# Raw sums of a scan's chunks on two column tiles, with six rearranging transfers per chunk

## The chip, the cores and the metric

The kernel runs on one core of a Trainium2 chip. The metric is the device time of one execution in microseconds, as the median of several runs. The core has TensorE (PE, whose weight loads are listed as PEld), VectorE (DVE), ScalarE (ACT), GpSimd (POOL) and SyncE (SP). SP and ACT issue the DMA transfers.

## The reference, cut to what matters

The input `x` is 32 sequences of 256 positions of 256 values. The output is `x + FFN(COND(x))`. `FFN` is two layers of windowed attention and a gated feed-forward part. `COND` is a state-space block, and the change lies in it:

```
xr, gate = split(x @ W_in.T);  xc = silu(conv4(xr + cond))
xn = layernorm(xc) * ln_g + ln_b                  # per position, 512 channels
Bm, Cm, dt = split(xn @ W_xproj.T, 3)             # 16 states each
dt = tanh(dt @ W_dt.T + b_dt) * 0.01;  Ad = 1 - dt * tanh(A_log)
Bd = Bm * min(norm(xn), 1)
h  = clip(h * Ad + Bd * xn, -10, 10)              # one step per position
y  = sum over states of Cm * h + D * xn
out = (y * silu(gate)) @ W_out.T
```

## The kernel before

The 32 sequences go in four groups of 8 (`GB`). A group's scan runs over 256 positions in 8 chunks of 32 steps (`CH`), so there are 32 chunks in all. On the partitions lie 16 states times 8 sequences, and `step` (line 719) does one position of all of them with one VectorE instruction of 128x512. Before it, `load_rows` (L688) loads the position's normalised rows, repeated over the 16 states, from DRAM into `xrep` on SP's queue, and `scale_row` (L708) scales them by `beta` on ScalarE, two steps ahead. `read_out` (L729) multiplies four steps' `h` on four 32-column tiles of TensorE into `y`.

What a chunk needs ahead of its steps is prepared about a chunk earlier. `conv_in` to `conv_out` make `xc`, which holds 512 channels as four blocks of 128 partitions, with 8 sequences times 32 steps as 256 columns. Three things follow from `xc`:

- `raw_sums` (L517) multiplies it with the 64 columns of `wx_sb` (16 each for Bm, Cm and dt, and 16 of zeros), in four fp32 matmuls of 256 columns, one per block of channels, each recorded as two passes. `raw_copy` (L526) copies the 64x256 sums from PSUM to `raw` on ScalarE. `raw_turn` (L531) brings them with three transfers on ScalarE's queue into `rw`, which has states times sequences on the partitions and three rows of 32 steps.
- `norm_turn` (L542) to `norm_put` transpose `xc`, normalise it and store it to DRAM as `xnd`, which `load_rows` reads back.
- `figures` and `figures_out` bring each position's scale, shift and norm to the layout of `rw`. `figures_in` (L633) is the first reader of `rw`: it makes `bcd` and `beta`. `decays` makes the running products, the limits and the read-out weights.

Group 0 runs its scan almost alone. Beside it TensorE projects the inputs of the other three groups ahead (`ahead_project`, L423, with `ps_a`) and spreads some rows itself (`spread_rows`, L693, with `bx`). From then on each group's scan runs beside attention and feed-forward of the group before it. After the last scan only attention and feed-forward are left. `values` (L1281) of the attention computes `ov` with 64-column weights, two heads alternating between the lower and the upper 64 output partitions; its products have 256 columns for the first window of keys and 128 for the second. `sums` (L1263) uses four 32-column tiles.

The source writes down an order. A table of slots, one per step, says which function is called in which slot:

```
at(s0 - 25, raw_copy, c)
at(s0 - 24, raw_turn, c)
...
at(s0 - 7, figures_in, c)
...
at(s0 - 27, raw_sums, c)
```

Here `s0` is the chunk's first step. The framework then orders the instructions of each engine by its own plan, except for those marked `keep_in_program_order`, and adds the waits. All eight PSUM banks form one ring (`ps_w`, `bufs=8`), from which every matmul output takes a bank. `raw` has one buffer and `rw` has two. A second form of the program (`exact`) is chosen only for large attention scales and does not run here.

Of the kernel before, what the change touches and what calls it, by code (L numbers as in the profile page):

```python
# [10 lines left out]
FP = mybir.dt.float32  # L11
# [8 lines left out]
P = 128  # L20
# [4 lines left out]
NC_ = DI // P  # L25
NS = 16
GB = 8
CH = 32
# [45 lines left out]
def kernel(  # L74
# [29 lines left out]
    nc = tc.nc  # L104
# [58 lines left out]
    for j in range(NJ):  # L163
# [20 lines left out]
        out=mask_t[:, 0:W], in_=mask_t[:, 0:W], compare_op=ALU.is_ge, fill=MASKED_LOW,  # L184
# [3 lines left out]
        out=mask_t[:, W : 2 * W], in_=mask_t[:, W : 2 * W], compare_op=ALU.is_ge,  # L188
# [14 lines left out]
    wx_sb = const.tile([P, NC_, 4 * NS], FP, tag="wx_sb", name="wx_sb")  # L203
# [15 lines left out]
    for i in range(2):  # L219
        t = const.tile([P, NI * (P + GB)], FP, tag=f"ly{i}", name=f"ly{i}")  # L220
# [3 lines left out]
    def program(ctx, exact):  # L224
        rpool = ctx.enter_context(tc.tile_pool(name="res", bufs=1, reuse_waits="tile"))
        wpool = ctx.enter_context(tc.tile_pool(name="weights", bufs=1, reuse_waits="tile"))
        sp = ctx.enter_context(tc.tile_pool(name="sp", bufs=1, reuse_waits="tile"))
# [6 lines left out]
        ps_w = ctx.enter_context(tc.tile_pool(name="psw", bufs=8, space=PSUM, reuse_waits="tile"))  # L234

        def bank(pool, tag, name):
            return pool.tile([P, DI], FP, tag=tag, name=name)
# [141 lines left out]
        def group_scan(g):  # L379
# [12 lines left out]
            ck = [{} for _ in range(NCH)]  # L392
# [122 lines left out]


            def raw_sums(c):  # L517
                pr = bank(ps_w, "w", "ps_raw")
                for ch in range(NC_):
                    nc.tensor.matmul(  # L520
                        pr[0 : 4 * NS, 0 : GB * CH], wx_sb[:, ch, :], ck[c]["xc"][:, ch],
                        start=(ch == 0), stop=(ch == NC_ - 1),
                    )
                ck[c]["pr"] = pr

            def raw_copy(c):  # L526
                raw = sp.tile([4 * NS, GB * CH], FP, tag="raw", name="raw")
                nc.scalar.copy(raw, ck[c].pop("pr")[0 : 4 * NS, 0 : GB * CH])
                ck[c]["raw"] = raw

            def raw_turn(c):  # L531
                rw = sm.tile([P, 3, CH], FP, tag="rw", name="rw")
                raw = ck[c].pop("raw")
                for i in range(3):
                    nc.scalar.dma_start(
                        out=rw[:, i],
                        in_=raw[i * NS : (i + 1) * NS].rearrange("n (b t) -> n b t", b=GB),
                    )
                ck[c]["rw"] = rw


# [320 lines left out]
            for c in range(NCH):  # L862
# [14 lines left out]
                for ch, s in enumerate((13, 16, 17, 18)):  # L877
                    at(s0 + s + 2, gate_th, c, ch)
                    if not alone:
                        at(s0 + s + 4, gate_out, c, ch)  # L880
                at(s0 - 25, raw_copy, c)
                at(s0 - 24, raw_turn, c)
                for j in range(NJ):
                    s = s0 - 26 + 4 * j
# [17 lines left out]
            for c in range(NCH):  # L902
                s0 = c * CH
                at(s0 - 43 if alone else s0 + 6, load_x, c)
                if alone:
                    for ch in range(NC_):
                        at(s0 - 40 + 2 * ch, project, c, ch)
                else:
                    for i in range(2):
                        at(s0 - 44 + 2 * i, load_projected, c, i)  # L910
                for ch, s in enumerate((13, 16, 17, 18)):
                    at(s0 + s, project, c, NC_ + ch)
                at(s0 - 27, raw_sums, c)
                for j in range(NJ):
                    at(s0 - 26 + 4 * j, norm_turn, c, j)
                at(s0 - 8, figures_out, c)
                for t in range(CH):
                    if not by_tensor(t):
                        at(s0 + t - 6, load_rows, c, t)
                    if by_tensor(t) and t % XR == 0:  # L920
                        at(s0 + t - 4, spread_rows, c, t)
                    at(s0 + t - 2, scale_row, c, t)
                for hb in range(CH // TB):
                    s = s0 + hb * TB
                    at(s - 9 if alone else s + 7, load_skip, c, hb)
                    at(s + 23, out_turn, c)
                for d in range(KM):
                    at(s0 + 43 + 2 * d, project_y, c, d)

            if alone:  # L930
                n = (NG - 1) * NCH * 2
# [130 lines left out]
        if exact:  # L1062
# [4 lines left out]
                out=mask[:, 0:W], in_=mask[:, 0:W], compare_op=ALU.is_ge, fill=MASKED,  # L1067
# [3 lines left out]
                out=mask[:, W : 2 * W], in_=mask[:, W : 2 * W], compare_op=ALU.is_ge, fill=MASKED,  # L1071
# [495 lines left out]
        for t in range(max(stages) + 1):  # L1567
# [3 lines left out]
            g, r = divmod(t + 1 + group - reload, group)  # L1571
# [124 lines left out]
```

## Time and profile before

| | us |
|---|---|
| median of 3 runs | 3545.7 |
| lowest and highest of the 3 | 3537.46, 3548.12 |
| the profiled execution, its own time | 3535.63 |
| the profiled execution, its span | 3533.5 |
| PE busy | 3418.2 |
| DVE busy | 2683.2 |
| ACT busy | 2035.4 |
| raw sums (L520), PE busy | 65.7 |
| copy of the raw sums (L528), ACT busy | 11.6 |

The profile shows one execution. Its busy times are unions of instruction spans for each engine, and issues of DMA transfers do not count as busy. A matmul record's duration holds a tail that the next one overlaps, so the distance from start to start says more than the duration. Times in the views are counted from the start of the span. In a group of instructions, `128*64` is the size of the weights (rows times columns of the array) and `128x256` that of the moving operand; `<-` names what ended a wait.

### The profile page before, as it was taken

To read this page: it belongs to the slowest core of one execution; us is meant where nothing else is said; L and a number is where in the kernel's file an instruction comes from. 1 tells how busy PE (TensorE), PEld (TensorE's weight loads), DVE (VectorE), ACT (ScalarE), POOL (GpSimd) and SP (SyncE) were. 2 spreads that over 40 slices of the span, in tenths; PEclk is the share of its full clock that TensorE was granted. 3 is DMA by queue.
4 is the path that set the end of the run, shared out by engine and by line. 5 is a ranking of instruction groups with operands and counts; after the bars stand their busy time and mean duration, and the time that the engine had idled before them with its cause. 6 is when DMAs were issued, how large, how long until landed. Compare 5 with 4: busy or idle time off the path is not lost.

```text
span 3533.5 us, 56484 instructions
## 1 busy us (share of the span) xinstructions
PE 3418.2 (97%) x19580; PEld 2257.4 (64%) x19580; DVE 2683.2 (76%) x5177; ACT 2035.4 (58%) x3663; POOL 1625.6 (46%) x1587
## 2 busy tenths in 40 slices
PE   7999989999999999999999999999999999999999
PEld 4545335666666666666666666666666777777777
DVE  5888898878788788888888888888787655555563
ACT  4666656656666665666666656666566444444442
POOL 4433456544455555544455555544444434333441
PEclk9999999999999999999999999999999999999999
DMA  7787655545454555444454555544444212011111
GB/s 208 215 217 218 198 169 153 136 113 142 129 143 130 150 147 151 136 114 134 117 142 128 148 148 147 137 120 130 118 142 118 61 37 62 13 31 36 37 28 38
DMA packets 487195, 436.65 MB, mean 124 GB/s; under 512 B 247155, under 2 KB 326516, under 8 KB 486772
## 3 DMA queue, kind: packets, MB, share of 16 engines
q1 hardware_dynamic: 401426, 420.41, 42.2%
q10 hardware_dynamic: 85474, 12.53, 2.1%
q8 instruction: 157, 2.57, 0.3%
q14 instruction: 138, 1.13, 0.1%
HBM read 384.06 MB, written 47.19 MB: 122 GB/s over the span
## 4 chain that ended last, share of the span: by engine, by line
PE 63%; DVE 17%; DMA 7%; POOL 5%; ACT 4%; issue 3%; SPq 1%; ACTq 0%; DVEq 0%; POOLq 0%
PE ps_qkv L996 13%; PE pa L1405 13%; DVE h L722 7%; PE po_f L1432 6%; PE y L734 5%; PE ps_wo L1052 4%; PE ov L1289 3%; DMA xrep<-xnd 3%; PE ps_out L814 3%; PE ps_in L401 3%; PE sc L1232 3%; PE tr_qk L1041 2%; PE rs L1269 2%; PE ps_raw L520 2%; DVE acc L491 1%
## 5 line engine op out<-in xcount | busy, mean ns | idle before, releaser
L722 DVE CUSTOM_DVE_ANT_0 h<-h,xrep,lim 128x512 f32<-128x512 f32 x1024 | 917.2, 896 | 137.3 <-ACT xrep L712 93.4
L712 ACT ACTIVATE xrep<-xrep,beta 128x512 f32<-128x512 f32 x960 | 671.6, 719 | 265.5 <-DMA xrep<-xnd 178.2
L996 PE MATMUL ps_qkv<-qkv,res 128*128 128x512 f32 x1536 | 716.0, 601 | 26.6 <-DVE ag L1423 12.5
L1405 PE MATMUL pa<-hT,w 128*128 128x256 f32 (+1 forms) x2816 | 674.7, 382 | 5.1 <-DVE zT L805 5.1
L1405 PEld LDWEIGHTS pa<-hT,w 128*128 128x128 f32 (+1 forms) x2816 | 517.4, 188 | 145.4 <-issue 41.8
L1020 POOL TENSOR_TENSOR rot<-rot,swp 128x512 f32<-128x512 f32 x256 | 345.1, 1348 | 496.7 <-DVE swp L1017 465.9
L996 PEld LDWEIGHTS ps_qkv<-qkv,res 128*128 128x128 f32 x1536 | 282.0, 191 | 311.5 <-issue 247.0
L1026 POOL TENSOR_TENSOR rn<-ss,neg_half 128x8 f32<-128x8 f32 x256 | 457.6, 1788 | 0.0
L734 PE MATMUL y<-h,ly 128*32 128x512 f32 x2048 | 341.1, 606 | 15.7 <-DVE h L722 13.6
L1432 PE MATMUL po_f<-ag,w 128*128 128x256 f32 x1280 | 306.7, 387 | 3.8 <-DVE fo L1443 3.1
L1423 DVE SCALAR_TENSOR_TENSOR ag<-pa,b_sb,ag 128x256 f32<-128x256 f32 x320 | 151.5, 474 | 208.7 <-ACT ag L1416 208.7
L1009 ACT ACTIVATE sq<-ps_qkv,tiny 128x512 f32<-128x512 f32 x256 | 173.3, 685 | 186.3 <-PE ps_qkv L996 129.3
L1432 PEld LDWEIGHTS po_f<-ag,w 128*128 128x128 f32 x1280 | 235.3, 190 | 68.3 <-DVE pT L1260 12.9
L1416 ACT ACTIVATE ag<-pa,b_sb 128x256 f32<-128x256 f32 x320 | 150.0, 469 | 209.7 <-PE pa L1405 206.8
L1357 POOL TENSOR_TENSOR rstd<-ve,neg_half 128x2 f32<-128x2 f32 x64 | 46.5, 726 | 484.9 <-DVE ve L1355 484.8
L1052 PE MATMUL ps_wo<-oT,wo 128*128 128x256 f32 x1024 | 231.6, 379 | 0.0
L1012 DVE TENSOR_TENSOR rot<-ps_qkv,rc_sb 128x512 f32<-128x512 f32 x256 | 175.1, 684 | 71.8 <-ACT sq L1009 70.1
L491 DVE SCALAR_TENSOR_TENSOR acc<-xr,wc_sb,acc 128x256 f32<-128x256 f32 x384 | 183.1, 499 | 50.8 <-POOL acc L480 50.0
L1017 DVE TENSOR_TENSOR swp<-ps_qkv,rs_sb 128x256 f32<-128x256 f32 x512 | 191.8, 416 | 27.6 <-POOL rot L1020 27.5
L1052 PEld LDWEIGHTS ps_wo<-oT,wo 128*128 128x128 f32 x1024 | 194.5, 190 | 27.2 <-ACT th_g L774 0.8
L1032 DVE SCALAR_TENSOR_TENSOR rot<-rn,rot 128x512 f32<-128x512 f32 x256 | 205.7, 841 | 7.5 <-POOL rn L1026 7.5
L1244 ACT ACTIVATE pT<-sc 128x512 f32<-128x512 f32 x384 | 201.6, 601 | 8.2 <-PE sc L1232 6.1
(161 smaller groups left out, 5375.6 us busy)
## 6 DMA issues: line engine op xcount, KB each, us to landing
xrep<-xnd SPq DMA_DIRECT2D x960, 256.0 KB
rb<-inv SPq DMA_DIRECT2D x128, 256.0 KB
xnd<-xn SPq DMA_DIRECT2D x64, 256.0 KB
qkv<-in_wqkv_dram SPq DMA_DIRECT2D x24, 512.0 KB
ahead<-xs_a SPq DMA_DIRECT2D x48, 256.0 KB
xp<-ahead SPq DMA_DIRECT2D x48, 256.0 KB
xd<-xnd SPq DMA_DIRECT2D x192, 64.0 KB
w<-in_w_dram SPq DMA_DIRECT2D x80, 128.0 KB
```

The lines of the kernel that those rows point to most:

```text
L491: nc.vector.scalar_tensor_tensor(acc, xr[:, :, k : k + CH], wc_sb[:, ch, k : k + 1], acc, ALU.mult, ALU.add,)
L712: scaled = nc.scalar.activation(bx, ck[c].pop(("bx", t), bx), AF.Copy, scale=ck[c]["beta"][:, t : t + 1])
L722: nc.vector._custom_dve(TENSOR_ADD_SAT, out=h_new, in0=state["h"], in1=bx, s0=ck[c]["lim"][:, 0, t : t + 1], s1=ck[c]["lim"][:, 1, t : t + 1],
L734: nc.tensor.matmul(ck[c]["y", hb][32 * q : 32 * q + 32, :], ly[hb % 2][:, 32 * t : 32 * t + 32], ck[c].pop(("h", hb * TB + t)), start=(i = ...
L996: nc.tensor.matmul(ps, res[b][:, k, t0 : t0 + W], wt["qkv", a][:, k], start=(k == 0), stop=(k == KM - 1),)
L1020: nc.gpsimd.tensor_add(rot, rot, swp)
L1026: nc.gpsimd.tensor_tensor(rn, ss, neg_half, ALU.pow)
L1032: nc.vector.scalar_tensor_tensor(rot, bc(rn, 2, DH), 1e12, rot, ALU.min, ALU.mult)
L1052: nc.tensor.matmul(po[:, d], wt["wo", 0][:, c, d * P : (d + 1) * P], oT[:, c, :], start=(c == 0), stop=(c == NC_ - 1),)
L1244: nc.scalar.activation(p, banks[r], AF.Exp)
L1405: nc.tensor.matmul(dst[x], wt["w1", m][:, k, x], self.h[:, k], start=(k == 0), stop=(k == KM - 1),)
L1432: nc.tensor.matmul(self.po[:, d], wt["w2", 0][:, m, d * P : (d + 1) * P], self.ag[m], start=(m == 0), stop=(m == len(MCH) - 1),)
```

## The change

`raw_sums` splits each chunk's 32 steps into two halves. Each block of channels is multiplied in two matmuls of 128 columns (8 sequences times 16 steps), one for each half. The first half goes to output partitions 0 to 63, the second to 64 to 127, with the same weights. `raw` becomes 128 partitions by 128 columns, and one ScalarE copy still moves it. `raw_turn` issues six transfers in place of three, one for each half and each of the three rows; a transfer's contiguous runs are 16 values long in place of 32.

```diff
             def raw_sums(c):
-                pr = bank(ps_w, "w", "ps_raw")
+                pr = bank(ps_w, "w", "ps_raw")[:, 0 : GB * CH // 2]
+                halves = ck[c]["xc"].rearrange("p c (b h t) -> p c b h t", b=GB, h=2)
                 for ch in range(NC_):
-                    nc.tensor.matmul(
-                        pr[0 : 4 * NS, 0 : GB * CH], wx_sb[:, ch, :], ck[c]["xc"][:, ch],
-                        start=(ch == 0), stop=(ch == NC_ - 1),
-                    )
+                    for h in range(2):
+                        nc.tensor.matmul(
+                            pr[64 * h : 64 * h + 64],
+                            wx_sb[:, ch, :],
+                            halves[:, ch, :, h],
+                            start=(ch == 0),
+                            stop=(ch == NC_ - 1),
+                        )
                 ck[c]["pr"] = pr
 
             def raw_copy(c):
-                raw = sp.tile([4 * NS, GB * CH], FP, tag="raw", name="raw")
-                nc.scalar.copy(raw, ck[c].pop("pr")[0 : 4 * NS, 0 : GB * CH])
+                raw = sp.tile([P, GB * CH // 2], FP, tag="raw", name="raw")
+                nc.scalar.copy(raw, ck[c].pop("pr"))
                 ck[c]["raw"] = raw
 
             def raw_turn(c):
                 rw = sm.tile([P, 3, CH], FP, tag="rw", name="rw")
                 raw = ck[c].pop("raw")
-                for i in range(3):
-                    nc.scalar.dma_start(
-                        out=rw[:, i],
-                        in_=raw[i * NS : (i + 1) * NS].rearrange("n (b t) -> n b t", b=GB),
-                    )
+                for h in range(2):
+                    for i in range(3):
+                        r = 64 * h + i * NS
+                        nc.scalar.dma_start(
+                            out=rw[:, i, h * CH // 2 : (h + 1) * CH // 2],
+                            in_=raw[r : r + NS].rearrange("n (b t) -> n b t", b=GB),
+                        )
                 ck[c]["rw"] = rw
```

## The prediction

> **What bounds the kernel now.** I read the page first: the engine sums, then the chain that ended last.
>
> ```profile
> span 3533.5 us, 56484 instructions
> PE 3418.2 (97%) x19580; PEld 2257.4 (64%) x19580; DVE 2683.2 (76%) x5177; ACT 2035.4 (58%) x3663; POOL 1625.6 (46%) x1587
> PE 63%; DVE 17%; DMA 7%; POOL 5%; ACT 4%; issue 3%; SPq 1%; ACTq 0%; DVEq 0%; POOLq 0%
> ```
>
> TensorE is busy nearly throughout and carries most of the chain; ScalarE, which gets the added work, carries 4% of it. An average can hide stages, so next the busy time by stretch (columns: length, PE, PEld, DVE, ACT, POOL, clock, DMA).
>
> ```profile
> 60.00:390.00 330.00, 309.21 (x1364) 166.05 (x1363) 283.71 (x497) 215.06 (x395) 128.58 (x168) 0.95 0.79 216
> 390.00:600.00 210.00, 186.74 (x867) 82.03 (x867) 185.64 (x346) 131.49 (x239) 116.48 (x119) 0.95 0.60 168
> 600.00:2600.00 2000.00, 1954.41 (x11703) 1308.82 (x11702) 1647.38 (x3233) 1243.01 (x2263) 1011.98 (x956) 1.00 0.49 135
> ```
>
> From 600 to 2600 us the scan of groups 1 to 3 runs beside attention and feed-forward: PE is busy 97.7%, at full clock. That stretch is TensorE's. In the first 390 us group 0's scan runs almost alone, with DMA at 0.79, and there the chain is mixed:
>
> ```profile
> by line: PE ps_a L428 13.7%; DMA xrep<-xnd 13.2%; PE y L734 12.6%; DVE h L722 9.8%; PE ps_in L401 8.2%; PE bx L699 7.3%; PE ps_out L814 5.8%; issue 5.5%; ACT xrep L712 4.0%; PE ps_raw L520 3.6%; DMA xq<-xnd 2.7%; PE tp_x L550 2.0%; POOL acc
> ```
>
> The PE terms sum to 53%, loads of xrep and xq to 16%, ACT xrep to 4%. Where the raw sums lie, by the busy time of line 520 alone in these stretches:
>
> ```profile
> 60.00:390.00 330.00, 12.71 (x48) 5.66 (x48) 0.95 0.79 216
> 390.00:600.00 210.00, 8.62 (x32) 3.72 (x32) 0.95 0.60 168
> 600.00:2600.00 2000.00, 38.82 (x160) 20.26 (x160) 1.00 0.49 135
> ```
>
> Eight passes make a chunk (four matmuls, each recorded as two passes), so 20 of the 32 chunks lie in the stretch that TensorE bounds, 4 in the transition, 8 before 390 us (two of these ahead of 60).
>
> **The matmuls.** The timeline of TensorE at one chunk, and at the one place that already alternates two 64-column tiles, `values` (line 1289):
>
> ```profile
> 1472.30 1.94 PE L520 MATMUL ps_raw<-xc,wx_sb 128*64 128x256 f32 x8
> 1474.17 0.65 PE L550 MATMUL tp_x<-ident,xc 128*128 128x128 f32 x4
> ...
> 1477.25 1.89 PE L1405 MATMUL pa<-hT,w 128*128 128x256 f32 x8
> 1478.98 1.45 PE L996 MATMUL ps_qkv<-qkv,res 128*128 128x512 f32 x3
> ...
> 1037.08 2.82 PE L1289 MATMUL ov<-pT,v_sb 128*64 128x256 f32 x32
> 1039.83 0.66 PE L791 MATMUL tz<-ident,xd 128*128 128x128 f32 x4
> ```
>
> A chunk's raw sums hold TensorE from 1472.30 to 1474.17: 1.87 us. Eight 256-column passes on a whole array take 1.73 us (1477.25 to 1478.98), 0.216 each, so the 64-column tile runs at the same rate with half the array idle, and 0.14 us goes to entering and leaving. The 32 passes of `ov` are 16 of 256 and 16 of 128 columns; one after the other they would take 16 x 0.216 + 16 x 0.108 = 5.2 us, and they take 2.75. In the trace's single records the two tiles' passes start 7 ns apart, and pairs of 128-column passes follow each other after 109 ns. After the change a chunk is 16 passes of 128 columns in 8 such pairs: 8 x 0.109 + 0.15 = 1.02 us. Saved: 0.85 us per chunk, 27 us over 32.
>
> Two things of it the trace does not show: passes whose moving operand is read in runs of 16 elements with a step, and 8 such pairs in a row (`ov` has two in a row; line 1269, on four 32-column tiles, has four groups of 128 columns in a row at the same 109 ns). Bounds: the same 109 ns, or no overlap at all, 16 x 0.109 + 0.15 = 1.89 us and nothing saved. I take the first, since `ov` is nearest.
>
> A rule speaks against it. The number of weight loads doubles to 16 per chunk; in `ov` each is recorded at 137 ns, starts 2 ns after a matmul pass, and the pairs still follow each other every 109 ns, so the loads are hidden. The Trainium skill, "TensorE: Matmul & The Clock Gate", Part 3 (The mechanism), says that a weight load overlaps running matmuls only when it targets another row group, and two column tiles share theirs; by its 64/1.2 = 53 ns per load (an estimate from that page) 16 loads in the open would cost 0.85 us and take the whole gain. The row decides.
>
> How much of it reaches the end: in the 20 chunks of the bound stretch TensorE's stalls are 45.6 us in 2000, and in the single records none lies in the 12 us behind the raw sums of chunks 11 to 31, so the next work moves up: 20 x 0.85 = 17.0 us. In the transition (PE 89%) I take half: 4 x 0.43 = 1.7. Before 390 us I take PE's 53% of the chain: 8 x 0.85 x 0.53 = 3.6.
>
> **The copy.** 64x256 takes 363 ns; rows of 128x512 copies take about 580, so 0.85 ns per element, and 128x128 is estimated at 255. That is 3.5 us less on ScalarE in all, off the path: 0.
>
> **The transfers.** Six issues per chunk on ScalarE's queue in place of three, each of half the bytes in runs of 64 bytes in place of 128. ScalarE at the same chunk:
>
> ```profile
> 1474.27 0.36 ACT L528 COPY raw<-ps_raw 64x256 f32<-64x256 f32 x1 [1.05 <-PE ps_raw L520]
> 1474.54 0.72 ACT L712 ACTIVATE xrep<-xrep,beta 128x512 f32<-128x512 f32 x1
> 1474.67 2.24 ACTq L535 DMA_DIRECT2D rw<-raw  x3
> 1477.01 0.72 ACT L712 ACTIVATE xrep<-xrep,beta 128x512 f32<-128x512 f32 x1 [1.75 <-DVE h L722]
> ```
>
> One issue takes 620 ns (median of 96), so three more hold ScalarE 1.9 us longer per chunk, 60 us in all. Queued behind them are the scalings of `xrep` that feed `step` (two steps ahead), the evacuations of TensorE's banks and the norm's scaling. Cover: here ScalarE idles in any case, because the next `xrep` waits for the scan on VectorE; in the 4 us after the issues ScalarE's idle time is over 2 us in most chunks after 1000 us. At 791 and 886 us it is 0.1 us or less. Without the cover the price is 1.9 us per chunk. In the bound stretch I take two or three uncovered chunks that eight PSUM banks still buffer: 0, with 20 x 1.9 = 38 us as the other end.
>
> Before 390 us the steps follow each other twice as fast and ScalarE idles only 0.5 to 1.1 us in those 4 us (2 to 3 in 8). Also, the DMA records carry eight semaphores taken in turn (279 issues each); a transfer takes 4 to 5 us to land there, and around 106 to 112 us an issue goes out 10 to 20 ns after the landing of the one eight before it. Three more transfers take 3 x 4.2 / 8 = 1.6 us of that ring, and SP's `xrep` loads queue behind. Bounds per chunk: 0, and 1.9 + 1.6 = 3.5 us. As ACT and these loads make 20% of the chain, 0.7 by shares; the idle time absorbs some: I take 0.5, so 8 x 0.5 = 4 us lost.
>
> The landing itself is hidden: `figures_in` reads `rw` 23 to 28 us after the last issue in group 0 and some 65 us later on, and a transfer lands in 2.1 us (median of the later stretch). Up to three more semaphore waits on VectorE ahead of `bcd`, 21 to 50 ns each, are under 0.15 us per chunk on an engine that is not the bound: 0. The skill, "DMA: Bandwidth & Descriptors", Rules for kernel authors, advises against this split (small transfers should be joined; under 64 KB they are mostly overhead). That would cost nothing here as long as it concerns only landing.
>
> **Order.** The records show TensorE's order is not the source's: in chunks 3 to 10 other matmuls stand between the passes of one raw sum. Other instructions and three more transfers may change the order elsewhere. A better order can gain at most the 45.6 us of stalls in the bound stretch; as bound for a loss I take as much again. Value: 0.
>
> **Sum.** -17.0 - 1.7 - 3.6 + 4 = -18.3 us. The profiled execution took 3535.6 us, 2 above its span and 10 below the median of the three runs, 3545.7. From the median: 3528 us (3517 against the profiled one).
>
> **Rivals.**
> 1. Everything saved counts, group 0 included, and the transfers cost nothing: -27, 3518 us. For it: PE is 94% busy even before 390 us. Against: ScalarE's thin idle time there. 12%.
> 2. No overlap of the tiles (the stepped read, or the loads): 0 saved, 4 lost: 3546 to 3552. Against it: `ov`. 10%.
> 3. Group 0 pays the full ring and issue price, 8 x 3.5 = 28 us, in place of 4: +6, about 3551; with half that price, 3537. Mostly within 0.3%. 10%.
> 4. Slower: ScalarE's queue. The three issues sit in front of `xrep` scalings and bank evacuations; if the idle time now seen there is moved rather than filled, `h` is late, then `y`, and TensorE waits. Full price 32 x 1.9 = 61 us against 27 saved: +34, 3579. It ends above +0.3% once over 1.2 us of the 1.9 shows per chunk. For it: chunks 791 and 886 without idle time, and a single ScalarE queue for all evacuations. Against: 4% of the chain. A worse order would show in the same waits. 23%.
>
> **How the numbers follow.** This kernel's three runs spread 0.3%, about what a measurement can tell from no change: 10.6 us. The forecast (45%) and rival 1 (12%) are faster, 57%; rivals 2 and 3 make 20% of no change; rival 4 is 23%. The forecast's own range is 3521 to 3536. Downward, 3508 takes in rival 1 and the 10 us by which runs of one kernel differ; upward, 3558 takes in rivals 2 and 3 and the lower third of rival 4.
>
> **What would show it.** Right: line 520 as 512 passes of 128 columns, in pairs 7 ns apart, the block to the next matmul near 1.02 us; `raw` as 128x128 near 255 ns; 192 issues; PE busy from 600 us on down by some 17 us with the stretch shorter by that. Wrong: blocks of 1.9 us; DVE `h` waiting for ACT `xrep` far above its 93 us in all; chunks of group 0 over 49 us apart; new PE stalls behind the raw sums.

## The result, and the profile after

The change is slower: 3551.1 us as the median of 10 runs (3549.7 to 3567.8) against 3538.7 for the kernel before (10 runs, 3534.7 to 3548.1). The ratio on record is 1.0042, 95% interval 1.0029 to 1.0055, some 15 us; the two medians lie 12.4 us apart.

The profiled execution took 3557.2 us (span 3555.0), 6 above the median of its runs, and the profiled one of before 3535.6, 3 below its own. The stretches compared below therefore add up to 22 to 24 us and not to 15. A second profile of each kernel repeats each stretch within 4 us.

The page of the change, engine sums, then the chain that ended last:

```profile
span 3555.0 us, 57111 instructions
...
PE 3419.3 (96%) x19836; PEld 2261.0 (64%) x19836; DVE 2669.0 (75%) x5177; ACT 2026.2 (57%) x3663; POOL 1608.7 (45%) x1587
...
PE 59%; DVE 18%; DMA 9%; POOL 5%; ACT 4%; issue 4%; SPq 1%; ACTq 0%; DVEq 0%; POOLq 0%
```

TensorE lost share of the chain (63 to 59%), and DMA and VectorE gained it. The busy time by stretch (length, PE, PEld, DVE, ACT, POOL, clock, DMA) answers to the table of before:

```profile
60.00:390.00 330.00, 310.89 (x1409) 164.52 (x1409) 263.75 (x473) 208.12 (x389) 124.49 (x162) 0.95 0.80 210
390.00:600.00 210.00, 177.02 (x810) 76.26 (x809) 179.34 (x338) 121.69 (x224) 106.45 (x117) 0.92 0.60 168
600.00:2600.00 2000.00, 1942.89 (x11897) 1301.72 (x11896) 1647.78 (x3239) 1246.56 (x2279) 997.97 (x957) 1.00 0.51 135
```

In 390 to 600 us TensorE is busy for 177.0 us in place of 186.7, and VectorE gets through 338 instructions in place of 346: the work arrives later there. From 600 us on TensorE's busy share falls from 97.7 to 97.1%, where a gain by the forecast's way would have left the share and shortened the stretch.

The matmuls themselves, on TensorE's timeline at one chunk, and as groups of the page's kind:

```profile
1495.59 1.07 PE L741 MATMUL y<-h,ly 128*32 128x512 f32 x8
1496.59 1.09 PE L522 MATMUL ps_raw<-xc,wx_sb 128*64 128x128 f32 x16
1497.61 0.66 PE L557 MATMUL tp_x<-ident,xc 128*128 128x128 f32 x4
```

```profile
L522 PE MATMUL ps_raw<-xc,wx_sb 128*64 128x128 f32 x512 | 39.0, 283 | 0.4 <-ACT xc L501 0.4
...
L533 ACT COPY raw<-ps_raw 128x128 f32<-128x128 f32 x32 | 8.4, 262 | 8.2 <-PE ps_raw L522 8.1
```

A chunk's raw sums hold TensorE from 1496.59 to 1497.61, 1.02 us, where they held it for 1.87; so it is in chunks 10 to 31, while in most earlier ones other matmuls stand between the passes. Passes start in pairs 7 ns apart, the next pair 109 ns later. Line 520's 65.7 us of busy time became 39.0. This part does what it says.

The transfers are six, on ScalarE's queue. First ScalarE's timeline at that chunk, then what waited for the transfers' line in the whole span (engine, reader: us, times):

```profile
1497.73 0.27 ACT L533 COPY raw<-ps_raw 128x128 f32<-128x128 f32 x1 [0.21 <-PE ps_raw L522]
1497.89 0.72 ACT L719 ACTIVATE xrep<-xrep,beta 128x512 f32<-128x512 f32 x1
1498.02 6.38 ACTq L542 DMA_DIRECT2D rw<-raw  x6
1504.45 0.72 ACT L719 ACTIVATE xrep<-xrep,beta 128x512 f32<-128x512 f32 x1 [5.84 <-DMA rw<-raw]
```

```profile
L542 ACTq DMA_DIRECT2D rw<-raw x192: 552/611/1552, 28.0 to 2606.7; - x192
...
who waited for it (us, times):
  ACT xrep L719: 73.1, 14
  ACT xs_a L439: 7.6, 2
  ACT rs_sb L1284: 3.4, 1
```

The same view of the kernel before:

```profile
L535 ACTq DMA_DIRECT2D rw<-raw x96: 552/620/1394, 28.6 to 2580.6; - x96
...
  ACT xrep L712: 4.3, 3
  ACT stat L574: 2.1, 1
  ACT ag L1416: 1.3, 1
```

Before, the three issues took 2.24 us and ScalarE's idle time behind them was 7.7 us in all; now it is 84.1 us. Six issues at 0.61 us would take 3.7 us, and here they take 6.4. The single DMA records show the rest. The kernel's DMAs carry eight semaphores, taken in turn by whatever is issued, on SP or on ScalarE. At this chunk the six carry numbers 104, 107, 108, 100, 102 and 103; number 103 had last gone to an `xrep` load, which SP issued at 1500.64 and which landed at 1503.83, and the sixth issue went out at 1503.85. In 18 of the 21 chunks 11 to 31 the sixth issue goes out 20 or 21 ns after the landing of a load from SP's queue on its own semaphore, nearly always an `xrep` load. ScalarE, whose next work is to scale `xrep`, waits for a load that it doesn't need yet: here the work that stood behind the six was the scaling at 1504.45, and the load that landed at 1503.83 was scaled at 1510.58. From the first issue to the end of the last, these chunks take 6.48 us on average, against 2.14 before.

The scan waits for it too (`h` is the step; after the bar: busy us, mean ns, then idle time before it and what ended most of it; the kernel before first, then the change):

```profile
L722 DVE CUSTOM_DVE_ANT_0 h<-h,xrep,lim 128x512 f32<-128x512 f32 x1024 | 917.2, 896 | 137.3 <-ACT xrep L712 93.4
L729 DVE CUSTOM_DVE_ANT_0 h<-h,xrep,lim 128x512 f32<-128x512 f32 x1024 | 911.0, 890 | 172.4 <-ACT xrep L719 141.6
```

In the second profiles the last number is 106.2 before and 141.5 with the change.

TensorE, which bounds chunks 11 to 31, hardly waits longer for `h` there: 2.1 us in both profiles of before, 2.0 and 2.6 in those of the change. Its idle time in these chunks rises all the same, from 44 and 46 us to 55 and 56, and most of the rise, from 2.5 and 3.0 us to 9.2 and 9.0, is idle time that ended when ScalarE had done `xn`, the norm's scaling out of a PSUM bank. In the list of TensorE's waits from 1140 to 2660 us (total, times, longest) it is the change's third row; before, that pair stood at 0.8 us:

```profile
PE ps_qkv L1003 <- DVE ag L1430: 13.0, 13, 2.4
PE ps_qkv L1003 <- DVE xd L792: 8.5, 13, 0.7
PE ov L1296 <- ACT xn L588: 6.3, 9, 2.0
```

Where these us lie is read from the start of `h` at the first step of a chunk, in the single records:

| stretch | before, two profiles | change, two profiles | difference of means |
|---|---|---|---|
| up to the first step | 48.7, 46.9 | 54.8, 54.2 | +6.7 |
| chunks 0 to 7 (group 0) | 390.0, 393.1 | 401.5, 405.3 | +11.9 |
| chunks 8 to 10 (transition) | 235.9, 235.3 | 243.0, 244.9 | +8.4 |
| chunks 11 to 31 (bound stretch) | 2075.2, 2073.6 | 2072.1, 2069.7 | -3.5 |
| after the scan | 783.7, 783.6 | 783.6, 783.6 | 0 |

So there are two questions: why the bound stretch gives 3.5 us and not 17, and where 27 us come from in the first 690 us. In that first part the order of instructions also changed. Compared engine by engine in the records, 75 of TensorE's, 123 of ScalarE's and 96 of VectorE's instructions that start before 690 us stand elsewhere in the sequence; behind it TensorE's sequence is the old one but for 2, ScalarE's but for 44 and VectorE's but for 20.

### The profile page after: what moved, and what is told of

It reads as the page before. It is cut to its first block, busy times and chain, and to the rows that moved or that the text cites. A ratio compares the mean times of both kernels' runs of the same rounds, so it can differ in the third digit from the quotient of the medians.

```text
span 3555.0 us, 57111 instructions
## 1 busy us (share of the span) xinstructions
PE 3419.3 (96%) x19836; PEld 2261.0 (64%) x19836; DVE 2669.0 (75%) x5177; ACT 2026.2 (57%) x3663; POOL 1608.7 (45%) x1587
## 4 chain that ended last, share of the span: by engine, by line
PE 59%; DVE 18%; DMA 9%; POOL 5%; ACT 4%; issue 4%; SPq 1%; ACTq 0%; DVEq 0%; POOLq 0%
PE ps_qkv L1003 13%; PE pa L1412 12%; DVE h L729 7%; PE po_f L1439 6%; PE y L741 5%; DMA xrep<-xnd 4%; PE ps_wo L1059 4%; PE ov L1296 3%; PE ps_in L401 3%; PE sc L1239 3%; PE ps_out L821 2%; PE tr_qk L1048 2%; DMA xp<-ahead 2%; PE ps_a L428 1%; PE rs L1276 1%
## 5 line engine op out<-in xcount | busy, mean ns | idle before, releaser
L729 DVE CUSTOM_DVE_ANT_0 h<-h,xrep,lim 128x512 f32<-128x512 f32 x1024 | 911.0, 890 | 172.4 <-ACT xrep L719 141.6
L1033 POOL TENSOR_TENSOR rn<-ss,neg_half 128x8 f32<-128x8 f32 x256 | 460.5, 1799 | 0.0
L741 PE MATMUL y<-h,ly 128*32 128x512 f32 x2048 | 356.4, 614 | 16.8 <-DVE h L729 14.3
L1239 PE MATMUL sc<-qT,kT 64*128 64x128 f32 (+2 forms) x2304 | 198.1, 331 | 4.3 <-DVE swp L1024 3.6
```

The source lines that it names most:

```text
L729: nc.vector._custom_dve(TENSOR_ADD_SAT, out=h_new, in0=state["h"], in1=bx, s0=ck[c]["lim"][:, 0, t : t + 1], s1=ck[c]["lim"][:, 1, t : t + 1],
L741: nc.tensor.matmul(ck[c]["y", hb][32 * q : 32 * q + 32, :], ly[hb % 2][:, 32 * t : 32 * t + 32], ck[c].pop(("h", hb * TB + t)), start=(i = ...
L1033: nc.gpsimd.tensor_tensor(rn, ss, neg_half, ALU.pow)
L1239: nc.tensor.matmul(banks[r][k0 : k0 + mk, i, q0:q1], kT[rows, i0 + i, kw * W + k0 : kw * W + k0 + mk], qT[rows, i0 + i, kw * W + q0 : kw * ...
```

## The experiments

Two theories compete. The queue: six issues in a row hold ScalarE, and that costs what the matmuls save. The order: the framework's own ordering came out differently because the instructions changed, and the transfers matter little. The table holds what all runs gave. "Six" or "three" is the number of transfers per chunk, "hold" the mean time from a chunk's first issue to the end of its last in chunks 11 to 31, "h waits" VectorE's idle time that a scaled `xrep` ended, over the whole span; all in us, the stretches from one profile each, a dash where it was not taken. The ratios are those on record; the medians' own lie within 0.15% of them (e2 1.0061, e3 1.0068, the farthest off). As two profiles of one kernel differ by up to 4 us in a stretch, and by 13 in "h waits", smaller differences say little.

| kernel | hold | h waits | up to chunk 7's end | 8 to 10 | 11 to 31 | ratio to before, 95% |
|---|---|---|---|---|---|---|
| before | 2.14 | 93.4, 106.2 | 438.7, 440.0 | 235.9, 235.3 | 2075, 2074 | 1 |
| change | 6.48 | 141.6, 141.5 | 456.3, 459.5 | 243.0, 244.9 | 2072, 2070 | 1.0042 (1.0029, 1.0055) |
| e1: new matmuls, three | 2.14 | 108.4 | 458.8 | 236.1 | 2059 | 1.0007 (0.9995, 1.0019) |
| e2: old matmuls, six | 5.99 | 133.2 | 444.8 | 242.5 | 2082 | 1.0047 (1.0033, 1.0062) |
| e3: three of six on SP | 4.67 | 131.7 | 469.7 | 244.1 | 2067 | 1.0053 (1.0037, 1.0069) |
| e4: change in groups 1 to 3 | - | 124.3 | 445.3 | 243.3 | 2069 | 0.9999 (0.9986, 1.0012) |
| e7: e1 in groups 1 to 3 | 2.06 | 92.0 | 442.8 | 237.6 | 2056 | 0.9965 (0.9953, 0.9977) |
| e8: three, and three later | - | 93.9 | 454.9 | 242.5 | 2062 | 1.0047 (1.0032, 1.0061) |
| e9: change, old order | 6.34 | 165.1 | 460.5 | 239.9 | 2105 | 1.0145 (1.0130, 1.0160) |
| e10: e1, old order | 2.19 | 109.0 | 442.4 | 236.6 | 2062 | 0.9979 (0.9969, 0.9988) |
| e11: change, order of e2 | 6.59 | 141.0 | 449.6 | 243.3 | 2072 | 1.0029 (1.0017, 1.0042) |
| e12: old work, order of change | 2.17 | 98.5 | 447.6 | 243.8 | 2070 | 1.0045 (1.0029, 1.0060) |

**e1: the new matmuls, three transfers.** Two copies put the halves back into a 64x256 tile, and the transfers are the old ones.

```
-                raw = sp.tile([P, GB * CH // 2], FP, tag="raw", name="raw")
-                nc.scalar.copy(raw, ck[c].pop("pr"))
+                raw = sp.tile([4 * NS, GB * CH], FP, tag="raw", name="raw")
+                rh = raw.rearrange("n (b h t) -> n b h t", b=GB, h=2)
+                pr = ck[c].pop("pr").rearrange("p (b t) -> p b t", b=GB)
+                for h in range(2):
+                    nc.scalar.copy(rh[:, :, h], pr[64 * h : 64 * h + 64])
```

> The matmuls of the change (16 passes of 128 columns on two tiles), but two ScalarE copies of 64x128 bring the halves into the old 64x256 layout, so that three transfers on ScalarE's queue remain. Theory A (the three added issues hold ScalarE and the eight-semaphore ring, and that eats the gain): the gain of TensorE shows, 12 to 20 us under the kernel before, about 3519 to 3527 against 3539. Rival B (TensorE's shorter block moves nothing, because ScalarE and VectorE pace the stretch): within 5 us of the kernel before. Rival C (the planner's other order in the first 500 us costs it, whatever the transfers are): slower than the kernel before by 5 to 15 us, with the loss ahead of 700 us.

The bound stretch falls to 2059 us, 15.6 below before, and the transition returns to 236. The time is that of before (1.0007), since group 0 and what is ahead of it stay 19 us late. So the loss of the bound stretch and of the transition goes with the six transfers in this pair, and the loss ahead of it doesn't. The time is rival B's, but not for its reason: the bound stretch is theory A's, and the loss ahead of 700 us is rival C's.

**e2: the old matmuls, six transfers.**

```
-                for i in range(3):
-                    nc.scalar.dma_start(
-                        out=rw[:, i],
-                        in_=raw[i * NS : (i + 1) * NS].rearrange("n (b t) -> n b t", b=GB),
+                rh = raw.rearrange("n (b h t) -> n b h t", b=GB, h=2)
+                for h in range(2):
+                    for i in range(3):
+                        nc.scalar.dma_start(
+                            out=rw[:, i, h * CH // 2 : (h + 1) * CH // 2],
+                            in_=rh[i * NS : (i + 1) * NS, :, h],
```

> The matmuls and the copy of before, but six transfers on ScalarE's queue, each with half of the steps. Theory A: the whole price of the transfers without the gain, 20 to 35 us over the kernel before, with 10 to 15 us of it in the stretch that TensorE bounds. Rival B: the price lies in the first 500 us alone, 15 to 20 us over, and nothing in the bound stretch. Rival C (order): anything from 0 to 15 us over.

The six transfers alone cost 0.47%: 7.7 us in the bound stretch, 7 in the transition, 5 up to the end of chunk 7, of which 2.4 are in chunks 0 to 7 and 3.0 ahead of them. By the medians (22 us) that is theory A's total, but the bound stretch falls short of its 10 to 15. The framework's order changed here too. Who waited for the transfers' line in this kernel:

```profile
L537 ACTq DMA_DIRECT2D rw<-raw x192: 552/611/1763, 28.5 to 2604.2; - x192
...
who waited for it (us, times):
  ACT xrep L714: 88.1, 19
```

It is the same wait as in the change, with the old matmuls: in 18 of the 21 chunks the sixth issue again goes out some 20 ns after an `xrep` load has landed.

**e3: the second half's three transfers on SP's queue.**

```
-                        nc.scalar.dma_start(
+                        (nc.scalar, nc.sync)[h].dma_start(
```

> The change with the second half's three transfers issued on SP's queue, so that ScalarE issues three as before while the number of transfers stays six. Theory A1 (the time of issue on ScalarE's queue is what costs): 12 to 20 us under the change, at or under the kernel before. Rival A2 (the ring of eight semaphores and the transfers themselves cost): no better than the change, 3545 to 3560.

The bound stretch gains 4 us over the change (2067), but group 0 takes 420 us, the longest of all. There SP's `xrep` loads are on the chain, and three more issues stand in their queue; but the order changed more than in any other run (127 of TensorE's instructions ahead of 690 us stand elsewhere than before, against 75 in the change), and the two were not separated. Moving three issues to the other queue did not help, that is all it shows.

**e4: the change in groups 1 to 3 alone.** Group 0, whose scan runs almost alone, keeps the old forms.

```
+            raw_sums, raw_copy, raw_turn = (
+                (raw_sums_a, raw_copy_a, raw_turn_a) if alone    # the old forms
+                else (raw_sums_b, raw_copy_b, raw_turn_b)        # those of the change
+            )
```

> The change in groups 1 to 3 alone; group 0's eight chunks keep the matmuls, the copy and the three transfers of before. If the loss is group 0's (theory: +10 us in its chunks, and a different order there): 10 us under the change, about 3540. If the loss is in the bound stretch and the transition: as the change, 3548 to 3553.

Up to 350 us no instruction stands elsewhere than before, and the end of chunk 7 comes at 445.3, 13 us earlier than with the change. Transition and bound stretch are as with the change (243.3 and 2069). The time is that of before, about 3540 as the first theory had it.

**Both kernels again.**

> The kernel before once more, for a second profile of it: how far the lengths of the stretches (to the first step, chunks 0 to 7, 8 to 10, 11 to 31) repeat. If they repeat within 1 to 2 us, the 10 to 16 us that the changed kernels lose in chunks 0 to 7 are the kernels' own; if they differ by 5 us or more, a single profile can't place a loss of that size there.

> The change once more, for a second profile. The same question: chunks 0 to 7 at 401.5 us and 8 to 10 at 243.0 in the first profile; chunks 11 to 31 at 2072 us. The last should repeat within 2 us under either theory, as its order hardly differs.

Their stretches stand in the first table. The change's sequence is the same in both its profiles, and so are its losses.

**e7: e1's form in groups 1 to 3 alone.** The diff is e4's, with e1's forms as the second set.

> Two tiles, two ScalarE copies and three transfers in groups 1 to 3 alone; group 0 as before the change. Theory A (in the bound stretch the gain of TensorE reaches the end as soon as ScalarE has only three issues; group 0 loses by order and not by work): chunks 11 to 31 shorter by 16 us as in the run with three transfers, chunks 0 to 7 as before, 10 to 17 us under the kernel before, 3522 to 3530. Rival (the first 500 us lose whatever is done in groups 1 to 3): 3535 to 3545.

This version beats both kernels: 3525.9 us, 0.9965 of before (0.9953 to 0.9977). ScalarE at a chunk of it:

```profile
1470.22 0.55 ACT L560 COPY raw<-ps_raw 64x128 f32<-64x128 f32 x2 [0.21 <-PE ps_raw L546]
...
1470.79 2.36 ACTq L567 DMA_DIRECT2D rw<-raw  x3
1473.25 0.72 ACT L749 ACTIVATE xrep<-xrep,beta 128x512 f32<-128x512 f32 x1 [1.86 <-DMA rw<-raw]
```

The time and the bound stretch are as theory A had them or better. The second copy costs some 0.3 us of ScalarE and three issues are spared, so the `xrep` behind the transfers starts 3.0 us after the copy's start in place of 6.7 (1504.45 - 1497.73). The bound stretch is 2056, 18.7 us below before: that is the matmuls' gain. Some 5 us of it go again ahead of that (442.8 and 237.6).

**e8: the later half's three transfers eight slots later**, outside group 0.

```
+                if alone:
                     at(s0 - 24, raw_turn, c)
+                else:
+                    at(s0 - 24, raw_turn, c, (0,))
+                    at(s0 - 16, raw_turn, c, (1,))
```

> The change, but in groups 1 to 3 the second half's three transfers go out eight steps after the first half's. Theory A1 (what hurts in the bound stretch is the sixth issue's wait in the ring of eight semaphores, 3 to 4 us with ScalarE held): chunks 11 to 31 at 2056 to 2062 us, against 2072 with the change and 2075 before; 8 to 14 us under the change in all. Rival A2 (each issue's own 0.62 us hurts, wherever it stands): 2068 to 2073 us, as the change.

Still six transfers, but outside group 0 never six in a row. The framework's plan did not keep the eight steps, which are some 25 us there: in chunks 11 to 31 the fourth issue starts 0.7 to 5.3 us behind the third, mostly 5. At the chunk shown below three go out together and three one by one, with other work between; the last of them, not shown, starts at 1500.53.

```profile
1492.62 1.92 ACTq L543 DMA_DIRECT2D rw<-raw  x3
...
1499.03 0.55 ACTq L543 DMA_DIRECT2D rw<-raw  x1
...
1499.94 0.55 ACTq L543 DMA_DIRECT2D rw<-raw  x1
```

```profile
  ACT xrep L719: 17.5, 6
  ACT xs_a L439: 4.4, 1
  POOL stat L574: 4.2, 1
```

The waits for the transfers' line (second fence, the same view as for the change) fall from 84.1 to 26.1 us, the sixth issue goes out right behind a landing on its own semaphore in 4 of the 21 chunks in place of 18, `h`'s wait for `xrep` returns to 93.9, and the bound stretch to 2062, 9 of the 14 us between the change and e1 or e7. That speaks for the six in a row, more than their number, as what costs there. It is not shown by the time: the profiled execution, 3544.8 us, is the fastest of six with a median of 3554.2, and the ratio stays at 1.0047 where theory A1 had 8 to 14 us under the change. The first 690 us are those of the change.

**e9 to e12: the same work in another order.** Edges between neighbours on each engine, which add no wait across engines, hold every engine's sequence to that of another kernel; the raw sums, the copy and the transfers stand at the places of the old ones, in e9 the three added transfers right behind the old three. In outline:

```
+        for a, b in zip(chain, chain[1:]):    # the other kernel's order, engine by engine
+            tc.add_manual_dep(b, a.name, ...)  # same engine: an order, no semaphore
```

e9 is the change in the order of before, e10 is e1 in the order of before, e11 the change in the order of e2, e12 the kernel before in the order of the change.

> The change, with every engine's other instructions held in exactly the order that the kernel before has (extra edges of order between instructions, no added waits); the 16 matmuls, the copy and the six transfers stand where the 4 matmuls, the copy and the three transfers stood. Theory O (group 0 and the lead-in lose 17 to 19 us because the planner orders them differently): up to the end of chunk 7 the run needs 440 to 447 us, as the kernel before (439 and 440) or the run with six transfers alone (445), against 456 and 460 with the change; in all 10 to 15 us under the change, 3537 to 3545. Rival W (the work itself costs there: the tiles, the copy or the transfers): 454 to 460 us, and 3550 to 3560 in all.

> Two tiles, two ScalarE copies and three transfers in all 32 chunks, with every engine's other instructions held in the order of the kernel before. Theory O: up to the end of chunk 7 436 to 443 us, against 459 with the planner's own order; chunks 11 to 31 2056 to 2060; in all 15 to 22 us under the kernel before, 3516 to 3523. Rival W: 454 to 460 us up to the end of chunk 7, 3535 to 3542 in all.

> The change, with all other instructions held in the order that the planner gave to the kernel with the old matmuls and six transfers, which needed 445 us up to the end of chunk 7. Theory O (the change's loss of 17 to 19 us there is its own order, not its work): 442 to 449 us up to the end of chunk 7, and in all 8 to 15 us under the change, 3537 to 3544. Rival W (six transfers together with the tiles cost it in any order): 455 to 461 us there.

> The kernel before in its work (four matmuls, three transfers), with all other instructions held in the order that the planner gave to the change. Theory O: 451 to 460 us up to the end of chunk 7 although nothing of the work is new; in all 3545 to 3562. Rival W: 438 to 443 us there, 3533 to 3543 in all.

*Order matters.* e12 does exactly the work of before, with nothing exchanged but the sequence: it loses 8 us up to the end of chunk 7, 6.9 of them ahead of the first step and 1.3 in chunks 0 to 7, and 8 in the transition, the whole loss of the change in the transition, and ends at 1.0045. Its bound stretch is 2070, 5 us below before: there the change's order alone costs nothing. (Up to the end of chunk 7 it lies between theory O and rival W.) e10 does e1's work: 442.4 in place of 458.8 up to the end of chunk 7, 13.8 of the 16.4 us in chunks 0 to 7, and the time falls from 1.0007 to 0.9979 (3529, some 6 us above theory O's range).

*The six matter too.* e9 has the order of before from the first instruction to the last, and is the slowest of all: 460.5 up to the end of chunk 7, and 2105 in the bound stretch. Neither expectation had a time near its 3591. Set against e10, which holds the same order and differs in the copies and the transfers alone, it is the clearest test of the six: 18 us more up to the end of chunk 7, 3 in the transition, 43 in the bound stretch, 1.0145 against 0.9979. That is 2.0 us for each of the 21 chunks, from a hold that is 4.2 us longer. TensorE's idle time in these chunks is 77 us against 47, with 17 against 5 of it ended by ScalarE's `xn`, and 27 against 13 by VectorE's `ag`. Who waited for its transfers' line:

```profile
L588 ACTq DMA_DIRECT2D rw<-raw x192: 552/612/1397, 28.8 to 2638.9; - x192
...
who waited for it (us, times):
  ACT xrep L765: 129.8, 24
```

In the order of before, `xrep` waits for the transfers' line 24 times in place of 14. That the framework's own order leaves more room around the long hold is a guess from this. e11, in the order that came out with six transfers and the old matmuls, takes 449.6 up to the end of chunk 7, the least that the change's work took in any order; its time, 3550, is no better than the change's median, against 3537 to 3544 by theory O.

So neither theory holds alone, and the two costs don't add up: in the transition the change's order costs 8 us with the old work (e12), and the six transfers cost 4 in the old order (e9), but together they cost 8. How the 18.5 us up to the end of chunk 7 split stays open. Pairs that differ in order alone differ there by 8 us (e12 against before, nearly all ahead of the first step), 8 (the change against e11, 7.6 of it in chunks 0 to 7) and 16 (e1 against e10, with three transfers); the pair that differs in transfers and copies alone, e9 against e10, by 18.

## Why the prediction was wrong, by its own steps

Predicted were 3528 us, within 3508 to 3558, with 57% on faster. The measured 3551 lies in the range, on the side that had 23%: the time rose where the forecast had it fall.

- **The matmuls, 0.85 us saved per chunk: right.** The block takes 1.02 us as worked out from the pairs of `ov`; eight pairs in a row and a stepped operand cost nothing more. In this trace the 16 weight loads, about 137 ns each, stay hidden. The Trainium skill's sentence in "TensorE: Matmul & The Clock Gate", Part 3 (The mechanism), that a load overlaps running matmuls only on another row group, does not hold for these two column tiles. The same section also names a background weight buffer as a way to load ahead, and no run here shows whether that is what hides them. An estimate from that page (16 loads of 53 ns in the open) would make the block 1.87 us.
- **The bound stretch, -17.0 us: right for the matmuls.** With three transfers the 21 chunks 11 to 31 take 2059 (e1) and 2056 (e7) in place of 2074, 16 and 19 us less, where 21 x 0.85 is 18. In the order of before (e10) it is 12.
- **Copy and landing, 0 each: right.** 262 ns against 255. `bcd` starts 21 to 26 us after the last issue in group 0 (15 in chunk 0) and some 61 us later on, so landing is hidden.
- **Three added issues in the bound stretch, 0: the step that failed.** They cost 2071 - 2057 = 14 us there in the framework's own orders (7.7 with the old matmuls, e2), and 43 in the order of before, from whose trace the prediction had read its cover (e9 against e10), about the 38 us that it named as the other end. Two things were mis-sized. The hold was put at three issues of 0.62, 1.9 us; it grew by 4.3, because issues also wait for a semaphore, the sixth for 2.1 us on average. The prediction had seen the ring of eight in group 0, and priced it there alone. But the ring is turned by a burst as well as by a rate: six in a row plus what SP issues meanwhile come round to a load still under way. And the cover, 2 us of idle time on ScalarE, was compared with 1.9; against 4.3 it is short. Even against 1.9 it was short more often than the two or three chunks allowed: in the trace of before, chunks 12 to 18 all have less than 1.9 us idle in the 4 us behind the issues. Of those 4.3 us some 0.65 per chunk (14 / 21) reach the end, 2.0 in the order of before. How much of that is the wait for the semaphore and how much the issues' own time was not separated.
- **Before 390 us, -3.6 + 4, and the transition, -1.7: wrong.** Measured were +18.5 up to the end of chunk 7 and +8.4 in chunks 8 to 10. The +4 for group 0's transfers can't be called right or wrong: with the old matmuls six transfers cost 5 up to there (e2, 2.4 of it in chunks 0 to 7), in the order of before 18 (e9 against e10), and against e1 nothing. e4, with group 0 left as it was, gets 13 of the 18.5 back; so the loss there comes with the edit in group 0, by its work and its order together.
- **Order, 0 within 45.6: the other step that failed.** The prediction looked for a changed order in the bound stretch, where TensorE's order stayed the same, and took its bound from there. It changed in the first 690 us, where pairs of runs put it at 8 to 16 us up to the end of chunk 7 and, with the old work, at 8 in the transition.
- **Which rival came true.** Half of rival 4's mechanism: ScalarE's queue held in front of `xrep`, with the sign that it named, as `h` waited 141.6 and 141.5 us in place of 93.4 and 106.2. But in the bound stretch the way to TensorE was not `h` and `y`; of the work held up there, TensorE waited longer for the evacuation by `xn`, the other thing that rival 4 had put behind the issues. Its point of decision, 1.2 us per chunk, did not apply, as 0.65 with the loss of order and group 0 was enough. Rival 3, the ring and issue price in group 0 (28 us at full price), names 3551 us, the time measured, and that is luck: it had the whole gain of 17 us in the bound stretch, where 3.5 came, and 28 in group 0, where 18.5 came, part of it by order. Of the signs named, group 0's chunks of over 49 us came true (401.5 / 8 = 50.2), though the second profile of before has 49.1 as well, and PE's busy time from 600 us on fell (by 11.5 in the fixed 2000 us) without the stretch becoming shorter by that.
- **The base.** The three runs' median stood 7 us above the ten runs' (3545.7, 3538.7), so the same sum from the latter would have said 3520.

## What to carry to other kernels

Price a split transfer by the time that its issues hold the issuing engine, and look at the semaphores of the DMA records: in a burst, an issue can wait for a transfer of another queue, so compare the cover with the burst's whole hold, not with the sum of its issues. Take a gain on TensorE where the data allow it without touching a busy queue: here the halves were joined again by two small copies outside group 0 (e7), and the predicted gain of the bound stretch came out. In a kernel whose order is made by a framework, an edit of a few instructions can cost or gain more by order than by its work; holding the order (e9 with e10, e12) shows each for itself, though here the two did not add up.

## What the runs showed of the hardware that was not expected

- An issue on ScalarE's queue waited 0.6 to 3.7 us (2.5 on average over 18 chunks) for an unrelated load on SP's queue, and went out 20 ns after it landed: the two queues share the eight semaphores. The Trainium skill, "DMA: Bandwidth & Descriptors", Rules for kernel authors, advises to join small transfers; these runs agree (+0.47% for six in place of three in e2), but the six transfers' own landing stayed hidden, and the price was the time for which the issuing engine was held.
- Two 64-column tiles run 8 pairs of fp32 passes at 109 ns a pair, with 16 weight loads of about 137 ns each, recorded beside them, hidden.
- The lead-in to the first step took 54 to 55 us in the change against 47 to 49, and TensorE was granted half its clock for longer there (20.0 and 14.7 us in the change's two profiles, 3.7 and 1.0 in those of before). The change's +6.7 us ahead of the first step goes with that: with half of the time at half clock taken off, an estimate of the clock that was lost, the lead-in is 46.9 and 46.4 us before, 44.8 and 46.8 with the change, and 44.8 to 47.8 in all fourteen profiles. The same holds for e12, whose 8 us lie mostly there (lead-in 54.7, 14.7 at half clock). Whether the order brings the lower clock stays open: e4 and e7, whose instructions stand there as before's, had 6.9 and 6.8 us at half clock. In group 0's scan the clock can't be the main thing: e3's is the slowest with less time at half clock than before's (20.7 us against 33.8), and in the change (41.5 and 39.9 against 33.8 and 29.8) half of the difference is 4.5 of the 11.9 us.
